# Residual and outputs by 32x32 VectorE transposes instead of TensorE transposes, in a two-layer attention and expert network

## Chip, cores and metric

The kernel runs on one NeuronCore of one Trainium2 chip. The metric is the device time of one execution in microseconds. A NeuronCore has a matrix engine (TensorE, PE in the profile, whose weight loads are listed apart as PEld), a vector engine (VectorE, DVE), an activation engine (ScalarE, ACT), a general engine (GpSimd, POOL) and a queue engine that issues transfers (SyncE, SP). SBUF is the on-chip working memory of 128 partitions, PSUM the memory into which TensorE writes.

## Reference

All arithmetic is float32. The input has 8 batches of 256 channels and 32 x 32 = 1024 positions (tokens). Cut to what matters:

```python
# layer 0: x is (8, 256, 32, 32); 8 heads of 64; softmax over axis 1 (the queries)
xt = x.reshape(B, C, S).transpose(0, 2, 1)
qkv = (xt @ w_qkv + b_qkv).reshape(B, S, 8, 192)
q, k, v = jnp.split(qkv, 3, axis=-1)
attn = softmax(einsum('bihd,bjhd->bijh', q, k) / 8, axis=1)
res = einsum('bijh,bjhd->bihd', attn, v).reshape(B, S, 512)
x = res @ w_out + b_out + xt                  # the residual is the transposed input
# layer 1: t is (8, 1024, 256), token by token
t = t + attention(layer_norm(t), W)           # one head, width 256, softmax over keys
n = layer_norm(t)
t = t + n + top-2-of-8 experts(n)             # each: gelu(n @ w1[e] + b1[e]) @ w2[e] + b2[e]
out = t.transpose(0, 2, 1).reshape(8, 256, 32, 32)
```

Two transposes of whole batches are therefore needed: the input is stored by channels and added as a residual by tokens, and the result is made by tokens and stored by channels.

## The kernel before

Batches are treated one after the other. In `layer0(b)` the input `xT` lies by channels (128 partitions, 2 channel halves, 1024 tokens). Queries and keys of a pair of heads are projected (`project_pair`, L324), and a hand-written order of 32 steps (4 head pairs by 8 blocks of 128 keys) interleaves scores `psc` (L422), the two halves of the column maximum (L437, L446, VectorE), the exponential (L463, ScalarE), the division of the values by the sums (L477, L479, VectorE) and the product `po` (L499). The products of one head pair are copied by ScalarE into `res` (L517), which holds the attention result by channels: 4 groups of 128 channels by 1024 tokens. The projection of a next head pair is put into the steps named in `PROJECT`; the last of these is step (2, 1). To keep `po` in order TensorE waits for empty instructions on another queue (`relay`, L509): POOL for batch 0, SP for the others.

After the steps the residual is formed (L584 to L604): 16 TensorE transposes of 128 x 128 squares of `xT` into two PSUM tiles `pt_x` (L590), two VectorE additions of the bias `b_o` that write `t1` (L593), then for each of 8 blocks of 128 tokens 4 products `pr` of `res` with `wo` (L601, the tokens of the block being the stationary operand) and a VectorE addition to `t1` (L604). Every float32 product shows in the trace as two matmul records and two weight loads; a transpose shows as one of each. `t1` and all that follows from it have the token within its block on the partition, so block `i` holds tokens 128 i to 128 i + 127.

`attend(b)` is the one-head attention of layer 1. Its waits are filled with the first products of the next batch (class `Begin`: `project`, L302, and `values`, L361). `normed(b)` is the second norm, `dispatch(b)` sends the normalised tokens of batches 0 to 6 to rows sorted by expert in device memory. When the steps of layer 0 of batch 7 are done, `experts` runs all sorted blocks. Then batch 7 goes through `attend` and `dense` (all experts for all its tokens) while the class `Results` brings the expert results of the other seven batches back by gathers (L1093), adds them (L1115) and stores them. What is gathered, added and stored at which place is written in the table `PLACES`, as (blocks to add, blocks to gather, halves to store).

`store` (L1145 to L1157) turns a result into the layout of the output: for each channel half it transposes 8 squares on TensorE into a PSUM tile `pout` (L1152), copies them with ScalarE into `oT` (L1154) and sends 512 KB with one transfer (L1155), 128 partitions with 4 KB each. For batch 7 it is called twice, once for each half of the tokens, with 256 KB for each transfer.

A PSUM tile of the kind `big` has three buffers, which `pt_x`, `pout`, the scores, the projections and the transposes of `attend` share; a tile of the kind `acc` has two, shared by `po`, `pr` and `py`.[...]

Of the kernel before, what the change touches and what calls it, by code (L numbers as in the profile page):

```python
# [10 lines left out]
F32 = mybir.dt.float32  # L11
# [8 lines left out]
def kernel(  # L20
# [23 lines left out]
    nc = tc.nc  # L44
# [160 lines left out]
    b1T = const.tile([P, E * NFC], F32, name="b1T")  # L205
    nc.vector.tensor_copy(b1T, ps[:, : E * NFC])

    def bcast(t, n):

        return t.unsqueeze(2).to_broadcast([P, NT, n])  # L210
# [181 lines left out]
    def nothing(*_):  # L392
        pass

    def layer0(b, xT, begun, routing):

# [131 lines left out]
        for at in range(last + LAG + 1):  # L528
            g, j = steps[min(at, last)]

            early = at > LAG and j == 1 and (g, j) not in PROJECT
            if at <= last:
                with tc.issue_after(counted.ins) if counted else nullcontext():
                    score(at, 0, 0)
            if 0 < at <= last + 1:
                with tc.issue_after(counted.ins) if counted else nullcontext():
                    score(at - 1, 1, 1)
                second_max(at - 1, 1)
                soften(at - 1, 1)
            if at >= LAG:  # L540
                with tc.issue_after(counted.ins) if counted else nullcontext():
                    gather_values(at - LAG, 0)
                counted = None
            if at <= last:

                with tc.issue_after(seconds[1].ins) if 1 in seconds else nullcontext():
                    first_max(at, 0)
                score(at, 0, 1)
                score(at, 1, 0)
                second_max(at, 0)  # L550
                if not early:
# [12 lines left out]
            if early:  # L564
                with tc.issue_after(copied[0].ins), tc.issue_after(copied[1].ins):
                    soften(at, 0)
            if at <= last and (g, j) in PROJECT:
                with tc.issue_after(firsts[at, 1].ins), tc.issue_after(array.ins):
                    share(firsts[at, 1])
                    pair, pq, mm = project_pair(b, xT, g + 1)  # L570
                qks.append(pair)
                if g == 0:
                    with tc.issue_after(mm.ins), tc.issue_after(firsts[at, 1].ins):
                        counted = share(pq)
                if b == B - 1 and (g, j) == PROJECT[-1]:
# [5 lines left out]
            pass  # L581


        t1 = one.tile([P, NT, C], F32, tag="t1", name=f"t1_{b}")  # L584
        n = 1024 // C
        for i in range(0, NT, n):
            pt = big(f"pt_x_{b}_{i}")
            for j in range(n):
                for cc in range(NCC):
                    nc.tensor.transpose(  # L590
                        pt[:, j * C + cc * P : j * C + (cc + 1) * P], xT[:, cc, ts(i + j, P)], ident
                    )
            nc.vector.tensor_add(  # L593
                t1[:, i : i + n, :],
                pt.rearrange("p (j c) -> p j c", c=C),
                b_o.unsqueeze(1).to_broadcast([P, n, C]),
            )
        for i in range(NT):
            pr = acc(f"pr_{b}_{i}")
            for g in range(NPAIR):  # L600
                nc.tensor.matmul(  # L601
                    pr[:, :C], res[:, g, ts(i, P)], wo[:, g, :], start=(g == 0), stop=(g == NPAIR - 1)
                )
            nc.vector.tensor_add(t1[:, i, :], pr[:, :C], t1[:, i, :])  # L604
        return t1
# [430 lines left out]
    class Results:  # L1036
# [67 lines left out]
        def add(self):  # L1104
            at = self.added
            if at == len(self.units):
                return
            assert at < self.sent
            self.added += 1
            b, i = self.units[at]  # L1110
            n = at // NT
            gate = self.group.kept[b][0]
            total = self.totals[n]
            for k in range(2):
                nc.vector.scalar_tensor_tensor(  # L1115
                    total[:, i, :],
                    self.slot(at)[:, k, :],
                    gate[:, k, i : i + 1],
                    total[:, i, :],
                    ALU.mult,  # L1120
                    ALU.add,
                )
# [10 lines left out]
        def tick(self, place, behind=None):  # L1133
# [6 lines left out]
                self.gather(behind)  # L1140
            for _ in range(stored):
                if self.whole:
                    b, total, cc = self.whole.pop(0)
                    store(b, total, range(NT), [cc])

    def store(b, total, blocks, ccs=range(NCC)):

        n = len(blocks)
        for cc in ccs:
            pt = big(f"pout_{b}_{blocks[0]}_{cc}")  # L1150
            for at, i in enumerate(blocks):
                nc.tensor.transpose(pt[:, ts(at, P)], total[:, i, ts(cc, P)], ident)  # L1152
            oT = two.tile([P, S], F32, tag="qk1", name=f"oT_{b}_{blocks[0]}_{cc}")
            nc.scalar.copy(oT[:, : n * P], pt[:, : n * P])  # L1154
            nc.sync.dma_start(  # L1155
                out[b, ts(cc, P), blocks[0] * P : (blocks[0] + n) * P], oT[:, : n * P]
            )  # L1157

    def dense(b, t2, tick):

# [71 lines left out]
        def collect(e, n, hT):  # L1232
# [23 lines left out]
            if n == NH2 - 1 and e + NWB < E:  # L1256
                weights(e + NWB)
            if e == E - 1:
                store(b, t2, range(n * (NT // NH2), (n + 1) * (NT // NH2)))

        pending = None
        for at, (e, n) in enumerate((e, n) for e in range(E) for n in range(NH2)):
# [7 lines left out]

    begun = Begin(0, next_x)
    begun.all()
    prepare()
    routing = (nothing(_) for _ in ())
    for b in range(B):
        xT = next_x
        if b + 1 < B:
            next_x = load_x(b + 1)
        t1 = layer0(b, xT, begun, routing)
        if b + 1 < B:  # L1280
            begun = Begin(b + 1, next_x)
            t2 = attend(b, t1, begun.at)
# [52 lines left out]
```

## Time and profile before

| | |
|---|---|
| time, 3 runs | median 2432.24 us (2429.27 to 2434.94) |
| the profiled execution's own time | 2433.04 us |
| its span | 2431.3 us |
| PE busy | 2380.9 us, 98% |
| DVE busy | 1499.5 us, 62% |
| ACT busy | 952.8 us, 39% |
| POOL busy | 381.4 us, 16% |
| transposes of the residual, `pt_x` | 128 of 273 ns each, beside 16 additions of 1219 ns |
| transposes of the outputs, `pout` | 128 of 273 ns each, beside 18 copies (14 of 128 x 1024, 4 of 128 x 512) |
| products `pr` | 512 records of 379 ns, weight loads of 190 ns |
| transfers | 118.65 MB in 57368 packets on the hardware queue |

[...] The profiled execution's own time exceeds its span by 1.7 us, and is 0.8 us above the median of the runs.

### The profile page before, as it was taken

The numbers are of one execution on the slowest core, as the hardware profiler recorded it, in microseconds if no ns is written. First come the engines' busy times: TensorE is split into PE (matmuls) and PEld (weight loads), VectorE is DVE, ScalarE is ACT, GpSimd is POOL, SyncE is SP. The second block draws the span as 40 slices with busy tenths as digits, with TensorE's granted clock in tenths as the row PEclk, the third lists the DMA queues.
The fourth block names the chain that finished last, engine by engine and source line by source line (L and its number), as shares of the span: only waits on it lengthen the run. The fifth ranks groups of instructions, "written<-read, shape, count | busy, mean of one in ns | idle before, by whom it ended". The sixth has DMA issues, their size and how long they took to land.

```text
span 2431.3 us, 37154 instructions
## 1 busy us (share of the span) xinstructions
PE 2380.9 (98%) x14015; PEld 1320.7 (54%) x14015; DVE 1499.5 (62%) x3642; ACT 952.8 (39%) x1587; POOL 381.4 (16%) x383
## 2 busy tenths in 40 slices
PE   9999999999999999999999999999999999999799
PEld 3356534654465336633663356335643588885566
DVE  5674577567755775577557764776478653335543
ACT  3651366126612661166215631563256422221222
POOL 0000011001100010002000200020002144436542
PEclk9999999999999999999999999999999999999899
DMA  7993101000000000000000000000001266663442
GB/s 277 386 384 89 35 19 36 1 18 17 21 18 18 12 25 18 18 8 29 18 2 19 34 18 1 18 34 3 1 18 62 83 218 219 213 207 103 151 148 99
DMA packets 82556, 188.23 MB, mean 77 GB/s; under 512 B 13992, under 2 KB 23880, under 8 KB 80584
## 3 DMA queue, kind: packets, MB, share of 16 engines
q1 hardware_dynamic: 57368, 118.65, 13.5%
q0 software_dynamic: 25008, 67.20, 9.0%
q8 instruction: 111, 1.82, 0.3%
q14 instruction: 69, 0.57, 0.1%
HBM read 100.49 MB, written 110.90 MB: 87 GB/s over the span
## 4 chain that ended last, share of the span: by engine, by line
PE 91%; DVE 3%; ACT 2%; issue 1%; DMA 1%; another core or an unknown queue 1%; SPq 0%; ACTq 0%; DVEq 0%; POOLq 0%
PE psc L422 18%; PE po L499 18%; PE py L661 9%; PE ps L635 7%; PE pqk L324 7%; PE pr L601 5%; PE pv L361 4%; PE ph L982 4%; PE pe L1007 4%; PE pdy L1238 2%; PE px L620 2%; PE pqk L302 2%; PE pa L654 2%; PE pdh L1214 2%; PE pt_n L234 1%
## 5 line engine op out<-in xcount | busy, mean ns | idle before, releaser
L463 ACT ACTIVATE ex<-psc,nmax 128x1024 f32<-128x1024 f32 x512 | 570.0, 1114 | 305.0 <-DVE scrap L446 221.8
L422 PE MATMUL psc<-qk,qk 64*64 64x512 f32 x4096 | 574.7, 592 | 4.4 <-ACT ex L463 4.4
L499 PE MATMUL po<-ex,vs 64*64 64x512 f32 x4096 | 570.2, 591 | 3.8 <-DVE vs L479 3.0
L446 DVE TENSOR_SCALAR_CACHE_REDUCE scrap<-psc,nmax 128x512 f32<-128x512 f32 x512 | 384.5, 751 | 178.8 <-PE psc L422 152.4
L437 DVE TENSOR_REDUCE nmax<-psc 128x1 f32<-128x512 f32 x512 | 350.6, 685 | 9.3 <-PE psc L422 9.3
L422 PEld LDWEIGHTS psc<-qk,qk 64*64 64x64 f32 x4096 | 179.9, 132 | 280.2 <-ACT ex L463 133.6
L499 PEld LDWEIGHTS po<-ex,vs 64*64 64x64 f32 x4096 | 175.3, 132 | 273.2 <-DVE vs L479 80.5
L661 PE MATMUL py<-n,aT 128*128 128x256 f32 x1024 | 238.4, 386 | 6.8 <-DVE aT L656 4.0
L635 PE MATMUL ps<-nT,xa 128*128 128x512 f32 x512 | 236.0, 592 | 0.0
L661 PEld LDWEIGHTS py<-n,aT 128*128 128x128 f32 x1024 | 191.8, 191 | 70.9 <-DVE aT L656 42.0
L845 POOL DMA_INDIRECT rows<-n,d_at x112 | 108.8, 971 | 705.9 <-DVE nmax L437 703.4
L646 ACT ACTIVATE ex<-ps,nmax 128x1024 f32<-128x1024 f32 x64 | 71.3, 1113 | 351.5 <-DVE nmax L643 306.6
L776 POOL TENSOR_TENSOR t<-t,n 128x2048 f32<-128x2048 f32 x8 | 36.3, 4535 | 1032.0 <-issue 766.8
L324 PE MATMUL pqk<-xT,wqkv 128*128 128x512 f32 x384 | 171.2, 599 | 0.0
L666 DVE SCALAR_TENSOR_TENSOR t<-py,rs,t 128x256 f32<-128x256 f32 x64 | 30.9, 483 | 206.3 <-PE py L661 206.3
L635 PEld LDWEIGHTS ps<-nT,xa 128*128 128x128 f32 x512 | 93.5, 190 | 81.2 <-issue 75.1
L1093 POOL DMA_INDIRECT yk<-y,yat x112 | 108.5, 969 | 108.4 <-DVE t L1247 39.5
L324 PEld LDWEIGHTS pqk<-xT,wqkv 128*128 128x128 f32 x384 | 71.0, 190 | 99.8 <-issue 77.8
L289 ACT ACTIVATE qk<-pqk,b_qks 128x512 f32<-128x512 f32 x124 | 85.6, 690 | 96.2 <-PE pqk L324 79.9
L361 PE MATMUL pv<-wqkv,xT 128*128 128x512 f32 x256 | 119.7, 597 | 0.2 <-ACT wqkv L106 0.2
L643 DVE TENSOR_REDUCE nmax<-ps 128x1 f32<-128x1024 f32 x64 | 78.3, 1223 | 61.4 <-PE ps L635 58.5
L601 PE MATMUL pr<-wo,res 128*128 128x256 f32 x512 | 111.8, 379 | 0.0
(193 smaller groups left out, 2499.1 us busy)
## 6 DMA issues: line engine op xcount, KB each, us to landing
rows<-wb SPq DMA_DIRECT2D x7, 8192.0 KB
y<-yb SPq DMA_DIRECT2D x63, 256.0 KB
xT<-in_x_dram SPq DMA_DIRECT2D x7, 1024.0 KB
sums<-t SPq DMA_DIRECT2D x7, 1024.0 KB
o<-sums SPq DMA_DIRECT2D x7, 1024.0 KB
out_dram<-oT SPq DMA_DIRECT2D x14, 512.0 KB
wpack<-in_L_ffn_w_dram SPq DMA_DIRECT2D x4, 1024.0 KB
wb<-in_L_ffn_w_dram SPq DMA_DIRECT2D x16, 256.0 KB
```

The costliest lines, as they stand in the source:

```text
L324: mm = nc.tensor.matmul(pq[:, ts(n, 512)], wqkv[:, cc, t, ts(g, P)], xT[:, cc, ts(n, 512)], start=(cc == 0), stop=(cc == NCC - 1),)
L361: nc.tensor.matmul(pv, self.xT[:, cc, ts(i, P)], wqkv[:, cc, 2, :], start=(cc == 0), stop=(cc == NCC - 1),)
L422: mm = nc.tensor.matmul(pss[at, h][ts(c, DK), ts(n, 512)], k[r, j * P + c * DK : j * P + (c + 1) * DK], q[r, ts(n, 512)], start=True, stop ...
L437: firsts[at, h] = nc.vector.tensor_reduce(nmax, pss[at, h][:, ts(0, 512)], AX.X, ALU.max, negate=True)
L446: seconds[h] = nc.vector.tensor_scalar(scrap, pss[at, h][:, ts(1, 512)], -1.0, nmaxes[at, h], ALU.mult, ALU.min, accum_out=nmax,)
L463: nc.scalar.activation(ex, pss.pop((at, h)), AF.Exp, bias=nmaxes.pop((at, h)), scale=1.0, accum_out=sums[at][:, h : h + 1],)
L499: mm = nc.tensor.matmul(po[n][ts(h, DK), :], vss[at][keys, h, :], exps[at, h][keys, ts(n, 512)], start=(j == 0 and turn == 0), stop=(j == ...
L601: nc.tensor.matmul(pr[:, :C], res[:, g, ts(i, P)], wo[:, g, :], start=(g == 0), stop=(g == NPAIR - 1))
L635: nc.tensor.matmul(psc[:, ts(n, 512)], xa[:, ec, ts(i, P)], nT[:, ec, ts(n, 512)], start=(ec == 0), stop=(ec == NCC - 1),)
L661: nc.tensor.matmul(py[:, :D], aT[:, ts(m, P)], n1[:, m, :], start=(m == 0), stop=(m == NT - 1))
L845: scatter = nc.gpsimd.indirect_dma_start(out=view[:, :], out_offset=bass.IndirectOffsetOnAxis(ap=ats[k][:, i : i + 1], axis=0), in_=n2[:, ...
L1093: ins = nc.gpsimd.indirect_dma_start(out=self.slot(at)[:, k, :], out_offset=None, in_=self.group.y[:, :], in_offset=bass.IndirectOffsetOnAxis(
```

## The change

The 256 TensorE transposes are gone, with the ScalarE copies and the PSUM tiles that belonged to them. VectorE transposes instead, an instruction of 128 x 1024 elements that transposes each 32 x 32 square within its group of 32 partitions. What such squares leave undone (moving a square to other partitions) is done by the transfers, and the order of the tokens within a half batch is changed so that transfers find runs of 128 tokens (512 bytes): partition 32 a + p of block `i` in half `n` holds token 512 n + 128 a + 4 p + i.

- `load_squares(b)` loads the input a second time, with 8 transfers of 128 KB (32 partitions by 8 by 128 elements), into the buffer that `attend` uses as `xa`.
- `residual(b, xs)` makes `t1` with two VectorE transposes, which read every fourth element of `xs`, and adds the bias with one POOL addition of 128 x 2048 elements. It is called in step (2, 1), behind the first maximum of that step.
- The stationary operand of `pr` is `own(res[:, g, :], i)`: 128 tokens at a distance of 4 elements (16 bytes), where it was 128 adjacent ones.
- `store(b, total, n)` stores one half of the tokens with one VectorE transpose, which writes every fourth element of `oT`, and four transfers of 128 KB.
- In `PLACES` the stores that stood at "last weights", "last products" and "norm 2" stand at ("mixed", 3) to ("mixed", 6), one half each.

```diff
+    NB = NT // NH2
+    SQ = 32
+    NQ = P // SQ
+    def own(t, i):
+        return t.rearrange("c (n p i) -> c n i p", n=NH2, i=NB)[:, i // NB, i % NB, :]
...
+    def load_squares(b):
+        xs = one.tile([P, C // SQ, NH2, P], F32, tag="xa", name=f"xs_{b}")
+        src = x[b].rearrange("(g c) (n a k) -> a n c g k", c=SQ, n=NH2, a=NQ)
+        for a in range(NQ):
+            for n in range(NH2):
+                nc.sync.dma_start(xs[ts(a, SQ), :, n, :], src[a, n])
+        return xs
+    def residual(b, xs):
+        t1 = one.tile([P, NT, C], F32, tag="t1", name=f"t1_{b}")
+        for n in range(NH2):
+            nc.vector.transpose(
+                t1[:, ts(n, NB), :].rearrange("p i (g c) -> p i g c", c=SQ),
+                xs[:, :, n, :].rearrange("p g (t i) -> p i g t", i=NB),
+            )
+        nc.gpsimd.tensor_add(t1, t1, b_o.unsqueeze(1).to_broadcast([P, NT, C]))
+        return t1
...
                 qks.append(pair)
+                if (g, j) == PROJECT[-1]:
+                    with tc.issue_after(firsts[at, 1].ins):
+                        t1 = residual(b, xs)
...
-        t1 = one.tile([P, NT, C], F32, tag="t1", name=f"t1_{b}")
-        n = 1024 // C
-        for i in range(0, NT, n):
-            pt = big(f"pt_x_{b}_{i}")
-            for j in range(n):
-                for cc in range(NCC):
-                    nc.tensor.transpose(
-                        pt[:, j * C + cc * P : j * C + (cc + 1) * P], xT[:, cc, ts(i + j, P)], ident
-                    )
-            nc.vector.tensor_add(
-                t1[:, i : i + n, :],
-                pt.rearrange("p (j c) -> p j c", c=C),
-                b_o.unsqueeze(1).to_broadcast([P, n, C]),
-            )
         for i in range(NT):
             pr = acc(f"pr_{b}_{i}")
             for g in range(NPAIR):
                 nc.tensor.matmul(
-                    pr[:, :C], res[:, g, ts(i, P)], wo[:, g, :], start=(g == 0), stop=(g == NPAIR - 1)
+                    pr[:, :C], own(res[:, g, :], i), wo[:, g, :], start=(g == 0), stop=(g == NPAIR - 1)
                 )
...
-            **{("mixed", i): (3, 2, 0) for i in range(1, 7)},
-            "last weights": (0, 0, 2),
-            "last products": (0, 0, 1),
+            **{("mixed", i): (3, 2, 1 if i > 2 else 0) for i in range(1, 7)},
             ("mixed", 7): (0, 2, 0),
-            "norm 2": (0, 0, 1),
...
-                self.whole += [(b, total, cc) for cc in range(NCC)]
+                self.whole += [(b, total, n) for n in range(NH2)]
...
-    def store(b, total, blocks, ccs=range(NCC)):
-        n = len(blocks)
-        for cc in ccs:
-            pt = big(f"pout_{b}_{blocks[0]}_{cc}")
-            for at, i in enumerate(blocks):
-                nc.tensor.transpose(pt[:, ts(at, P)], total[:, i, ts(cc, P)], ident)
-            oT = two.tile([P, S], F32, tag="qk1", name=f"oT_{b}_{blocks[0]}_{cc}")
-            nc.scalar.copy(oT[:, : n * P], pt[:, : n * P])
-            nc.sync.dma_start(
-                out[b, ts(cc, P), blocks[0] * P : (blocks[0] + n) * P], oT[:, : n * P]
-            )
+    def store(b, total, n):
+        oT = two.tile([P, D // SQ, P], F32, tag="qk1", name=f"oT_{b}_{n}")
+        nc.vector.transpose(
+            oT.rearrange("p g (t i) -> p i g t", i=NB),
+            total[:, ts(n, NB), :].rearrange("p i (g c) -> p i g c", c=SQ),
+        )
+        dst = out[b].rearrange("(g c) (n a k) -> n a c g k", c=SQ, n=NH2, a=NQ)
+        for a in range(NQ):
+            nc.sync.dma_start(dst[n, a], oT[ts(a, SQ)])
...
     begun.all()
+    xs = load_squares(0)
     prepare()
...
+        if b > 0:
+            xs = load_squares(b)
-        t1 = layer0(b, xT, begun, routing)
+        t1 = layer0(b, xT, begun, routing, xs)
```

More of the change, by code (lines that the diff above doesn't have):

```diff
@@ L393, in nothing, with layer0 @@
         pass
-    def layer0(b, xT, begun, routing):
+    def load_squares(b):
[14 more added lines that the diff above has]
+        return t1
+    def layer0(b, xT, begun, routing, xs):
         v, qks = begun.v, begun.qks
@@ L1142, in tick @@
                 if self.whole:
-                    b, total, cc = self.whole.pop(0)
-                    store(b, total, range(NT), [cc])
-    def store(b, total, blocks, ccs=range(NCC)):
-        n = len(blocks)
-        for cc in ccs:
-            pt = big(f"pout_{b}_{blocks[0]}_{cc}")
-            for at, i in enumerate(blocks):
-                nc.tensor.transpose(pt[:, ts(at, P)], total[:, i, ts(cc, P)], ident)
-            oT = two.tile([P, S], F32, tag="qk1", name=f"oT_{b}_{blocks[0]}_{cc}")
-            nc.scalar.copy(oT[:, : n * P], pt[:, : n * P])
-            nc.sync.dma_start(
-                out[b, ts(cc, P), blocks[0] * P : (blocks[0] + n) * P], oT[:, : n * P]
-            )
+                    b, total, n = self.whole.pop(0)
+                    store(b, total, n)
+    def store(b, total, n):
[7 more added lines that the diff above has]
+            nc.sync.dma_start(dst[n, a], oT[ts(a, SQ)])
     def dense(b, t2, tick):
@@ L1258, in collect @@
             if e == E - 1:
-                store(b, t2, range(n * (NT // NH2), (n + 1) * (NT // NH2)))
+                store(b, t2, n)
         pending = None
```

## The prediction

> **What bounds the kernel now.** First the page's busy times and its chain of waits.
>
> ```profile
> PE 2380.9 (98%) x14015; PEld 1320.7 (54%) x14015; DVE 1499.5 (62%) x3642; ACT 952.8 (39%) x1587; POOL 381.4 (16%) x383
> ...
> PE 91%; DVE 3%; ACT 2%; issue 1%; DMA 1%; another core or an unknown queue 1%; SPq 0%; ACTq 0%; DVEq 0%; POOLq 0%
> ```
>
> TensorE is the path: 91% of the chain. What is taken off it counts unless a wait is beneath; transfers and POOL matter only through waits. Next the timeline where batch 1 leaves layer 0 (start, duration, engine, line; brackets are idle time).
>
> ```profile
> 416.50 0.44 PE L590 MATMUL pt_x<-ident,xT 128*128 128x128 f32 x2
> ...
> 417.26 2.32 PE L499 MATMUL po<-ex,vs 64*64 64x512 f32 x16 [0.32 <-DVE vs L479]
> ...
> 419.52 1.75 PE L590 MATMUL pt_x<-ident,xT 128*128 128x128 f32 x14
> 419.63 1.08 ACT L517 COPY res<-po 128x512 f32<-128x512 f32 x2 [2.99 <-PE po L499]
> ...
> 421.10 3.19 PE L601 MATMUL pr<-wo,res 128*128 128x256 f32 x14
> ```
>
> Fourteen residual transposes fill 419.52 to 421.10, but the copies of `po` to `res` run beneath them. Then the timeline of step (2, 1), batch 1, where the residual goes.
>
> ```profile
> 357.54 7.13 PE L324 MATMUL pqk<-xT,wqkv 128*128 128x512 f32 x16
> ...
> 357.86 0.68 DVE L437 TENSOR_REDUCE nmax<-psc 128x1 f32<-128x512 f32 x1
> ...
> 365.76 0.75 DVE L446 TENSOR_SCALAR_CACHE_REDUCE scrap<-psc,nmax 128x512 f32<-128x512 f32 x1 [7.22 <-PE psc L422]
> ```
>
> VectorE has a hole of 7.22 us there, behind the maximum that `residual` is placed after. The last stage, by the timeline:
>
> ```profile
> 2256.33 1.91 PE L1152 MATMUL pout<-ident,o 128*128 128x128 f32 x16
> 2265.21 1.76 PE L654 MATMUL pa<-ident,ex 128*128 128x128 f32 x7 [6.97 <-ACT oT L1154]
> ...
> 2330.61 1.91 PE L1152 MATMUL pout<-ident,o 128*128 128x128 f32 x16
> 2332.36 3.60 PE L1214 MATMUL pdh<-n2T,wb 128*128 128x512 f32 x8
> ```
>
> Sixteen output transposes take 1.75 us from a dense stream (109 ns each); once TensorE also waits 6.97 us for the copies that free PSUM. Last, rows of the groups by shape, for costs:
>
> ```profile
> L601 PEld LDWEIGHTS pr<-wo,res 128*128 128x128 f32 x512 | 96.7, 190 | 12.8
> L688 PEld LDWEIGHTS pl<-n2T,rT 128*32 128x32 f32 x128 | 3.3, 111 | 7.7 <-DVE n2T L235 5.3 <-DVE o L1115 0.8 <-issue 0.4
> ...
> L816 DVE TENSOR_TENSOR d_rows<-d_rows,counts 128x64 f32<-128x64 f32 x6 | 1.3, 224 | 0.2
> L810 DVE TENSOR_TENSOR d_rows<-d_upto,d_per 128x64 f32<-128x64 f32 x7 | 1.9, 276 | 0.2
> L799 DVE COPY d_per<-d_cn 128x64 f32<-128x64 f32 x7 | 1.4, 207 | 0.0
> ```
>
> L810 writes at a distance of 32 bytes and takes 52 ns more than L816, which writes adjacent elements: 0.8 ns per element on top of one. L799 reads at that distance and takes 207 ns, less than either.
>
> [...]
>
> **The change part by part**, against the profiled execution's own 2433.0 us.
>
> *Residual off TensorE.* Without `pt_x`, `pr` still needs the PSUM buffer that the first `res` copy frees: it ends at 419.63 + 0.54 = 420.17, with a signal about 420.33. So `pr` starts 0.77 us earlier instead of 1.58. The instruction order of the new kernel puts four passes of the next batch's projection (0.215 us each, 0.87 us) around the last `po`, into the wait. But these passes came after `pr` and covered the norm: in the timeline of batch 1 `pt_n` starts at 440.07, straight after the projections, and the last `n` (L224, 437.11 + 2.67) is ready at 439.78: no slack. What is pulled forward is missed there. I take 0.77 x 8 = 6.2 us gained (13 if the norm chain gives way, 0 if the copies' wait grows).
>
> *Residual on VectorE.* Two transposes of 1024 elements: [...]like L593 (1.22 us), or about 2 us if the 16-byte reads cost what L810's writes do. 2.4 to 4 us fit in the hole of 7.22 us. The POOL addition costs 4.54 us by L776, the same shape; it ends by 367.1 at the latest if the transposes run 358.6 to 362.6, before the next two-input VectorE instruction, L479 at 368.32. `t1` is needed 55 us later; expert scatters wait behind the addition on POOL, and nobody waits for them soon. Batch 0: the order-keeping empty instructions stand behind it on POOL; with TensorE 6 us in the projection, 0.5 us (0 to 3). Batch 7: `plan` already fills the hole (TensorE waits 0.8 us for its last instruction, L906), so both transposes are exposed: 3 us (2.4 to 4).
>
> *Loading squares.* 8 MB more in all, on transfer engines that the page shows under 20% busy in these stages. SP issues the 8 transfers once the previous `attend` is through with `xa`, when the empty instructions of the new batch are not yet due; the data has 80 us to land. Nothing.
>
> *The strided weight load of `pr`.* This is the large unknown: 512 loads. The matmuls step at 0.2155 us, the load beneath takes 190 ns. From 32 to 128 columns it rises by 79 ns, 0.83 ns per column, so 107 of the 190 are columns. If columns cost nothing more, the load stays hidden. If the column part doubles, as L810's writes do, a full load takes 297 ns; its column part of 214 is still under the step if loads overlap one another (the transposes' loads of 141 ns at steps of 109 show that they can), and it adds (297 - 216) x 512 = 42 us if not. [...]Below nothing is excluded, since the load is already hidden. I take 2 us, because reads at a distance cost little in L799 and half rate just fits.
>
> *Outputs off TensorE.* In `dense` 80 of the 112 transposes lie in the dense stream: 80 x 0.109 = 8.7 us. In the last `attend` the first 16 cost 1.75 and the wait 6.97; the second 16 lie beneath VectorE's `aT` and save nothing. Part of the wait has a releaser that the profile doesn't know, so I take 7.5 of 8.7 us (2 to 10).
>
> *Outputs on VectorE.* Four transposes go into ("mixed", 3 to 6), beside 6.7 us of VectorE work per block (two of 1.22, six additions of 0.494, small ones of 1.25 in all) and 7.75 us of TensorE (8 x 0.109 + 8 x 0.43 + 16 x 0.2155): 1.22 or 2.1 us more make 7.9 to 8.8. They stand after `aT`, which TensorE awaits, and before the next maximum, which has a step's slack: 1 us lost in all (0 to 4). In `dense` VectorE idles over 4 us per step. Each store issues 4 transfers instead of 1 (0.34 us each on SP): hidden.
>
> *Around the gates.* Without copies ScalarE's order changes: a first Gelu slips ahead of the exponential of the gates, with table loads of 1.28 us. That chain ends in `pg`, for which TensorE waits 2.48 us already: 1.5 us (0 to 3).
>
> *The end.* The chain shows 0.44 + 0.53 us of transposes for the first half of batch 7 within the last products; they go (0.97). The last store trades 0.87 us of transposes and two copies of 0.5 us for one VectorE transpose (1.2 to 2.1 us), four issues instead of two, and packets of 512 bytes instead of 2 KB: 2 us lost, 1 net (0 to 3).
>
> *Sum:* -6.2 + 0.5 + 3 + 2 - 8.7 - 7.5 + 1 + 1.5 + 1 = -13.4, to 2433.0 - 13.4 = 2419.6; the median stands 0.8 lower: 2419.
>
> **Rivals.** *A, the forecast:* 2419. With the bounds of its small terms 2407 to 2429. *B, the gain drowns:* the waits beneath persist: `attend` keeps its 7 us in another place, the boundary gains nothing. -8.7 of `dense` against the 9 us of costs above: 2432. For it: most of the gaps in that stage have unknown releasers; against it: the dense stream is without idle time. *C, weight loads don't overlap:* `pr` steps at 297 ns, 2419 - 2 + 42 = 2459, slower. It decides from 248 ns on, where 512 x 32 ns eat the gain. For it: the cost of L810. Against: a half-rate column part is 214 ns. *D, [...]:* 2419 - 2 + 109 = 2526. For it: nothing reads weights in steps in this trace, so it is open; against: L799.
>
> **How the numbers follow.** A 0.57, B 0.11, C 0.19, D 0.13. No change is within 0.2%, 4.9 us, about what a measurement can tell. A lies wholly below 2427 but for little: faster 0.60 with the part of B that keeps the wait's gain; same 0.06; slower 0.34 (C, D, a little of B). The predicted time is A's. A's own range is 2407 to 2429; for 8 in 10 the range must take in B and most of C: 2407 to 2465. D is left out above.
>
> **What would show it.** The start-to-start step of `pr`: 0.2155 us says A, about 0.3 C, over 0.4 D; its loads' mean in the groups: under 300 ns fits A or C. The VectorE transposes' mean: 1.2 or 2. The window of step (2, 1): no TensorE idle time except in batch 7. TensorE's time from the last `po` to `pt_n`: 0.8 us shorter. `pdh` following `pdy` without a gap in `dense`, and no wait of 7 us at the last two blocks of `attend`. I am wrong if the `pr` stage grows by more than 2 us per batch, or if VectorE's transposes take over 3.5 us and overflow their hole.

## The result, and the profile after

The change takes 2423.06 us (median of 6 runs, 2419.51 to 2426.44) where the kernel before, run beside it, takes 2433.37 us (6 runs, 2429.27 to 2435.03): a ratio of 0.9957, interval 0.9946 to 0.9968, some 10 us. The profiled execution of the change took 2419.76 us, its span is 2418.1 us, 13.2 us less than that of before. The forecast of 2419 us was 4 us low. Most of its terms were not right, though, and the experiments were made to find out which.

The page of the change, busy times and the chain of waits:

```profile
PE 2363.3 (98%) x13759; PEld 1315.7 (54%) x13759; DVE 1546.1 (64%) x3658; ACT 939.3 (39%) x1570; POOL 419.0 (17%) x391
...
PE 91%; DVE 5%; ACT 2%; issue 1%; another core or an unknown queue 1%; DMA 1%; SPq 0%; DVEq 0%; ACTq 0%; POOLq 0%
```

256 matmul records are gone, and TensorE is busy 17.6 us less; VectorE's share of the path rose from 3% to 5%. Its groups by shape (line, engine, operation, shape, count | busy us, mean ns | idle us before) show what was bought and what it cost:

```profile
L619 PE MATMUL pr<-wo,res 128*128 128x256 f32 x512 | 121.6, 398 | 0.3 <-ACT res L546 0.3
L619 PEld LDWEIGHTS pr<-wo,res 128*128 128x128 f32 x512 | 120.7, 331 | 3.7 <-ACT res L546 3.7
...
L417 DVE STREAM_TRANSPOSE t<-xs 128x1024 f32<-128x1024 f32 x16 | 32.0, 2064 | 0.0
...
L1164 DVE STREAM_TRANSPOSE oT<-o 128x1024 f32<-128x1024 f32 x14 | 28.6, 2040 | 0.2
```

The weight loads of `pr` take 331 ns instead of 190, and each VectorE transpose about 2 us, the upper of the two values that the prediction considered. The timeline where batch 1 leaves layer 0 (TensorE alone):

```profile
416.42 2.35 PE L528 MATMUL po<-ex,vs 64*64 64x512 f32 x16
418.70 1.13 PE L311 MATMUL pqk<-xT,wqkv 128*128 128x512 f32 x2
419.66 15.18 PE L619 MATMUL pr<-wo,res 128*128 128x256 f32 x64
434.67 1.88 PE L311 MATMUL pqk<-xT,wqkv 128*128 128x512 f32 x4
436.39 1.88 PE L370 MATMUL pv<-wqkv,xT 128*128 128x512 f32 x4
438.11 1.93 PE L243 MATMUL pt_n<-ident,n 128*128 128x128 f32 x16
```

Passes of the next projection (`pqk`) now fill the wait for the copies of `po`. The 64 records of `pr` start at a distance of (434.67 - 419.66) / 64 = 0.2345 us instead of 0.2155. So the loads of 331 ns overlap one another here, but not without cost: 19 ns for each of 512 records, 9.7 us in all. Batch 7 in step (2, 1), where VectorE also runs `plan`, a chain of small instructions that lays out the experts' blocks; first the kernel before, then the change:

```profile
1856.73 0.17 DVE L877 TENSOR_TENSOR_SCAN p_ends<-ones,p_blocks 128x8 f32<-128x8 f32 x1
...
1861.62 0.19 DVE L906 CAST row_at<-p_lo 128x63 int32<-128x63 f32 x1
```

```profile
1852.04 4.04 DVE L417 STREAM_TRANSPOSE t<-xs 128x1024 f32<-128x1024 f32 x2
...
1856.22 4.73 POOL L421 TENSOR_TENSOR t<-t,b_o 128x2048 f32<-128x2048 f32 x1 [2.85 <-issue]
...
1857.02 3.96 DVE L895 TENSOR_TENSOR_SCAN p_ends<-ones,p_blocks 128x8 f32<-128x8 f32 x1
...
1865.70 0.20 DVE L924 CAST row_at<-p_lo 128x63 int32<-128x63 f32 x1
...
1867.91 1.99 PE L451 MATMUL psc<-qk,qk 64*64 64x512 f32 x8 [6.07 <-ACT ex L492]
```

The scan of 8 elements took 0.17 us before and takes 3.96 us here; it ends 0.03 us after POOL's addition (1860.98 against 1860.95 us). The plan ends at 1865.9, 14.8 us after TensorE began the projection of this step (1851.1), where before it took 7.1 us (1854.8 to 1861.8): 4 us of transposes and 3.8 us of the scan. TensorE waits 6.07 us for what stands behind it. In the other batches the same pieces are hidden, as in step (2, 1) of batch 1:

```profile
357.33 3.99 DVE L417 STREAM_TRANSPOSE t<-xs 128x1024 f32<-128x1024 f32 x2
...
361.46 4.54 POOL L421 TENSOR_TENSOR t<-t,b_o 128x2048 f32<-128x2048 f32 x1 [2.80 <-issue]
...
364.62 0.75 DVE L475 TENSOR_SCALAR_CACHE_REDUCE scrap<-psc,nmax 128x512 f32<-128x512 f32 x1 [3.30 <-PE psc L451]
```

VectorE still idles 3.30 us of its hole of 7.22. In the last stage, from the norm of batch 7 to `pg`, the view of waits (total, times, longest, in us) gives for TensorE:

```profile
PE pt_n L243 <- DVE rstd_f L231: 4.0, 1, 4.0
PE py L679 <- DVE aT L674: 3.7, 2, 2.7
PE plT L729 <- ACT lT L714: 3.1, 1, 3.1
PE py L679 <- issue: 2.6, 1, 2.6
```

The wait of 6.97 us for `oT` is gone, but waits of similar kinds remain.

The two traces compared by stretches, from the starts of the same products; the prediction's terms are put where they belong. A boundary is the passage from layer 0 of a batch to its norm. A second pair was taken later on one chip (below).

| stretch (us, change minus before) | predicted | first pair | second pair |
|---|---|---|---|
| start to the norm of batch 6 (7 boundaries) | -3.2 | -4.1 | -3.7 |
| from there to the last `po` of batch 7 (the plan) | +3.0 | +8.8 | +9.4 |
| from there to the norm of batch 7 (last boundary, experts) | -0.5 | -2.0 | +0.6 |
| from there to `pg` (last `attend`, gates) | -5.0 | -6.0 | -3.2 |
| from `pg` to the end | -7.7 | -9.9 | -11.3 |
| sum | -13.4 | -13.2 | -8.2 |

### The profile page after: what moved, and what is told of

Its sections match the earlier page's. It is cut to its first block, busy times and chain, and to the rows that moved or that the text cites. A ratio compares the mean times of both kernels' runs of the same rounds, so it can differ in the third digit from the quotient of the medians.

```text
span 2418.1 us, 36817 instructions
## 1 busy us (share of the span) xinstructions
PE 2363.3 (98%) x13759; PEld 1315.7 (54%) x13759; DVE 1546.1 (64%) x3658; ACT 939.3 (39%) x1570; POOL 419.0 (17%) x391
## 4 chain that ended last, share of the span: by engine, by line
PE 91%; DVE 5%; ACT 2%; issue 1%; another core or an unknown queue 1%; DMA 1%; SPq 0%; DVEq 0%; ACTq 0%; POOLq 0%
PE po L528 19%; PE psc L451 18%; PE py L679 9%; PE ps L653 8%; PE pqk L333 7%; PE pr L619 5%; PE ph L1000 4%; PE pe L1025 4%; PE pv L370 4%; PE px L638 2%; PE pdy L1251 2%; PE pa L672 2%; PE pdh L1227 2%; PE pqk L311 2%; PE px L990 1%
## 5 line engine op out<-in xcount | busy, mean ns | idle before, releaser
L619 PEld LDWEIGHTS pr<-wo,res 128*128 128x128 f32 x512 | 120.7, 331 | 3.7 <-ACT res L546 3.7
L619 PE MATMUL pr<-wo,res 128*128 128x256 f32 x512 | 121.6, 398 | 0.3 <-ACT res L546 0.3
```

What stands on the lines that cost most here:

```text
L619: nc.tensor.matmul(pr[:, :C], own(res[:, g, :], i), wo[:, g, :], start=(g == 0), stop=(g == NPAIR - 1))
```

## The experiments

The theory after the first reading: the strided weight loads cost 9.8 us, POOL's addition beside the plan another 4, and the rest of the gain is what the TensorE transposes were worth. Each run below has its own runs of the kernel before on its chip; times are medians, and the chips differ (the kernel before took 2433.8 us beside the first four, 2418.1 beside the next four, 2432.8 beside the last four), so ratios are compared.

### Runs of adjacent tokens

The token of partition 32 a + t in block i becomes 128 a + 32 i + t within its half. The copy out of PSUM puts the tokens in that order, and all else reads and writes adjacent elements. This kernel is called e1_runs below.

```diff
-        return t.rearrange("c (n p i) -> c n i p", n=NH2, i=NB)[:, i // NB, i % NB, :]
+        return t[:, ts(i, P)]
...
-                xs[:, :, n, :].rearrange("p g (t i) -> p i g t", i=NB),
+                xs[:, :, n, :].rearrange("p g (i t) -> p i g t", i=NB),
...
-                copied = [nc.scalar.copy(res[:, g, ts(n, 512)], po[n]) for n in range(NH2)]
+                copied = [
+                    nc.scalar.copy(
+                        res[:, g, ts(n, 512)].rearrange("c (i a t) -> c a i t", i=NB, a=NQ),
+                        po[n].rearrange("c (a i t) -> c a i t", i=NB, a=NQ),
+                    )
+                    for n in range(NH2)
+                ]
...
-            oT.rearrange("p g (t i) -> p i g t", i=NB),
+            oT.rearrange("p g (i t) -> p i g t", i=NB),
```

> All of the change stays, but blocks of tokens are made of runs of 32 adjacent tokens instead of every fourth one: both VectorE transposes then read and write adjacent elements, and the copies of po to res write the tokens in the order in which the weight loads of pr read them, so these read adjacent elements. Theory 1 (the loads of pr cost more because of the distance of 16 bytes): loads back from 331 to about 190 ns, the step of pr from 0.2345 to 0.2155 us, 512 x 0.019 = 9.8 us less, 2413 us; if the distance also makes the VectorE transposes long (2.06 us), they fall to about 1.2 us and the plan of batch 7 and the end give another 2 us, 2411. Rival (the step of pr grew for another reason, such as a lower clock or the evictions): step stays at 0.2345, 2423 us. For the transposes: near 2.06 us means that fp32 squares cost that by themselves, near 1.2 that the distance does.

Measured: 2412.10 us, 0.9916 of before (0.9900 to 0.9933). The groups of this kernel by shape:

```profile
L625 PEld LDWEIGHTS pr<-wo,res 128*128 128x128 f32 x512 | 97.2, 190 | 16.7 <-ACT res L547 3.7
L547 ACT COPY res<-po 128x512 f32<-128x512 f32 x64 | 34.2, 588 | 28.9 <-PE po L528 28.9
...
L417 DVE STREAM_TRANSPOSE t<-xs 128x1024 f32<-128x1024 f32 x16 | 18.9, 1219 | 0.0
L1170 DVE STREAM_TRANSPOSE oT<-o 128x1024 f32<-128x1024 f32 x14 | 17.3, 1237 | 0.2
```

The loads are back at 190 ns, and the transposes take 1.22 and 1.24 us, about the duration of the addition that the lower estimate was read from (L593, 1.22 us). So a distance of 16 bytes is what cost 141 ns per load, 0.84 us per transpose when reading (L417) and 0.80 when writing. The reordered copy takes no longer than before: 588 ns in both kernels.

### Adjacent weights alone

```diff
-        return t.rearrange("c (n p i) -> c n i p", n=NH2, i=NB)[:, i // NB, i % NB, :]
+        return t[:, ts(i, P)]
```

> The change as it is, but pr reads its weights from adjacent tokens again, with the transposes' distance of 16 bytes kept. (The attention part of a token then meets the residual of another token: the computation is changed there.) Theory 1: pr's loads 190 ns, step 0.2155 us, 9.8 us less than with the change: 2413 us, with the VectorE transposes unchanged at 2.06 us. Rival (something other than the distance in the loads): loads 331 ns, 2423 us.

Measured: 2412.62 us, 0.9918 (0.9904 to 0.9933), with loads of 190 ns and transposes of 2058 and 2034 ns. This and the kernel above are equal within the intervals, so nearly all of the 10 us between the change and them is the weight loads, and the rival falls. What the shorter transposes of e1_runs bring is too little for the times to tell. In the traces it is 0.8 us in batch 7 (the stretch with the plan is 7.8 us longer than before in e1_runs, 8.6 here) and 0.8 us at the end (from the last `pdy` 7.4 us instead of 8.2); elsewhere none of it shows.

### Residual alone

`store`, the list of halves and `PLACES` as before the change, all else as in the change. The store of before doesn't undo the change's order of tokens.

```diff
-    def store(b, total, n):
+    def store(b, total, blocks, ccs=range(NCC)):
...
-            **{("mixed", i): (3, 2, 1 if i > 2 else 0) for i in range(1, 7)},
+            **{("mixed", i): (3, 2, 0) for i in range(1, 7)},
+            "last weights": (0, 0, 2),
+            "last products": (0, 0, 1),
...
+            "norm 2": (0, 0, 1),
```

> Residual by squares alone; outputs are transposed by TensorE as before (the tokens of the outputs come in another order). From the measured parts: the boundary gains 0.60 us in each of 8 batches (-4.8), pr costs +9.8, the plan of batch 7 about +6: slower than before by 11, 2444 us. By the prediction's own terms (-6.2 + 0.5 + 3 + 2) it would be 2433. If the gain that was seen came mostly from the residual, it would be under 2425.

Measured: 2440.03 us, 1.0026 (1.0014 to 1.0039): 6 us slower than before, where 11 were expected and the prediction's terms would give none. The expected loss was too large: the gain at the boundary is larger than the 0.60 us that the expectation took from the wait alone (see the point-by-point part).

### The addition written behind the plan

```diff
+                        if b < B - 1:
+                            bias(t1)
...
                         plan(groups[0])
+                        bias(t1)
```

> The change as it is, but in batch 7 POOL's addition of the bias comes after the plan, the VectorE transposes still ahead of it. Theory (POOL's addition and VectorE instructions with two SBUF inputs exclude each other): the scan p_ends falls from 3.96 to about 0.17 us, TensorE's wait at psc from 6.07 to about 2.3 us, 3.8 us less than with the change: 2419 us. Rival (the plan is late only because 4 us of transposes stand ahead of it): the wait stays near 6 us, 2423 us.

Measured: 2423.23 us, 0.9960 (0.9945 to 0.9975), as the change. The run says nothing about the theory: nothing in the data makes the addition wait for the plan, and POOL ran it as soon as the transposes were done, as the timeline of batch 7 shows:

```profile
1856.39 4.74 POOL L424 TENSOR_TENSOR t<-t,b_o 128x2048 f32<-128x2048 f32 x1 [2.83 <-issue]
...
1857.20 3.97 DVE L900 TENSOR_TENSOR_SCAN p_ends<-ones,p_blocks 128x8 f32<-128x8 f32 x1
```

### The addition made to wait for the plan

```diff
-                        plan(groups[0])
+                        planned = plan(groups[0])
+                        tc.add_manual_dep(bias(t1).ins, planned.ins.name, BEHIND)
```

> e1_runs, and in batch 7 POOL's addition of the bias now truly waits for the last instruction of the plan (in e4_add_after_plan it had only been written behind the plan, and ran at the same moment as before, so that run told nothing). Theory (POOL's addition and VectorE instructions with two SBUF inputs exclude each other): the scan p_ends falls from 3.96 to about 0.17 us and the plan ends some 3.8 us earlier; but the addition then lies beside the next vs of VectorE (a product of two SBUF inputs), which should stretch to 2 to 4 us in its turn, so that the time falls by between 0 and 3.8 us from 2412: 2408 to 2412. Rival (the scan is long for a reason of its own or because the queue of VectorE is long): the scan stays at 3.96 us.

Measured: 2394.86 us, 0.9911 (0.9897 to 0.9924), beside 0.9916 for the kernel that it was made from. The timeline of batch 7:

```profile
1846.81 0.17 DVE L906 TENSOR_TENSOR_SCAN p_ends<-ones,p_blocks 128x8 f32<-128x8 f32 x1
...
1852.62 4.53 POOL L424 TENSOR_TENSOR t<-t,b_o 128x2048 f32<-128x2048 f32 x1
...
1854.15 3.16 DVE L510 TENSOR_TENSOR vs<-v,rs 128x128 f32<-128x128 f32 x1
...
1857.37 1.09 PE L530 MATMUL po<-ex,vs 64*64 64x512 f32 x8 [2.36 <-DVE vs L510]
```

The scan is 0.17 us again and `vs`, 0.29 us elsewhere, is stretched to 3.16 us in its place, ending 0.16 us after POOL. The reductions of PSUM that ran on VectorE between the addition's start and `vs` kept their 0.7 us. So the stretch follows POOL's addition: moving it frees the scan (0.17 us) and stretches the two-input instruction that then lies beside it (`vs`, 3.16 us). TensorE's waits in e1_runs and here:

```profile
1857.94 1.99 PE L451 MATMUL psc<-qk,qk 64*64 64x512 f32 x8 [4.39 <-ACT ex L492]
```

```profile
1853.91 1.09 PE L453 MATMUL psc<-qk,qk 64*64 64x512 f32 x8 [0.60 <-ACT ex L494]
```

The 4.39 us behind the plan have become 0.60 there and the 2.36 at `po`. In the trace the stretch with the plan is 5.0 us longer than before, where it was 7.8; a gain in time over e1_runs is not shown, the ratios being equal within their intervals.

### The residual of batch 7 one step earlier

Made from e1_runs, and called e6_residual_earlier below.

```diff
-                if (g, j) == PROJECT[-1]:
+                if (g, j) == PROJECT[-1 if b < B - 1 else -2]:
```

> e1_runs, with the residual of batch 7 (transposes and POOL's addition) one projection step earlier, at (1, 1), where no plan stands; the other batches as in e1_runs. Theory (the plan of batch 7 pays for the transposes ahead of it and for POOL's addition beside it): the scan is 0.17 us again, TensorE's wait at psc behind the plan falls from about 6 us to about that of the kernel before, where the last wait there was 0.8 us, and the 7 to 8 us by which batch 7 fell behind come back: 2405 us. Rival (the loss of batch 7 has other causes, such as the lower clock seen after the wait): 2410 to 2412.

Measured: 2392.70 us, 0.9896 (0.9881 to 0.9912): the lowest ratio of the study together with the last variant below, though its interval overlaps that of e1_runs, so a gain over e1_runs is not shown by the times. In the trace the scan takes 0.17 us and the wait behind the plan is gone. From the norm of batch 6 to the last `po` this kernel falls behind the one before by 4.2 us, where e1_runs fell behind by 7.8. Left over is a stretch of the same kind with another victim, at (1, 1), where the expert routing of batch 6 runs; `d_rows`, 0.23 us in the kernel before, takes 4.54 us here and ends 0.09 us after POOL's addition:

```profile
1811.77 4.51 POOL L421 TENSOR_TENSOR t<-t,b_o 128x2048 f32<-128x2048 f32 x1 [49.26 <-DVE t L417]
...
1811.83 4.54 DVE L835 TENSOR_TENSOR d_rows<-d_rows,d_cn 128x64 f32<-128x64 f32 x1
...
1821.18 1.56 PE L451 MATMUL psc<-qk,qk 64*64 64x512 f32 x8 [2.40 <-ACT ex L492]
```

The next variant has the same code in this stretch and falls behind by only 2.5 us: there the wait is 2.42 us, but the records of `psc` and `po` after it take 1.09 and 1.04 us, here 1.56 and 1.95. So half to two thirds of the theory's 7 to 8 us came in the traces.

### The gates before the first Gelu

e6_residual_earlier, with the first Gelu of `dense` ordered behind the exponential of the gates, which saves a table load (1.28 us in the traces) within their chain.

```diff
-                now = (e, n, hidden(e, n))
+            with tc.issue_after(exped[0].ins) if at == 0 else nullcontext():
+                now = (e, n, hidden(e, n))
```

> e6_residual_earlier, and the first Gelu of the dense stage is ordered behind the exponential of the gates. Theory (the Gelu that slipped ahead cost the chain of the gates a table load of 1.28 us): about 1.2 us less than e6_residual_earlier, pg's wait on all_gates shorter by as much. Rival (pg waits for VectorE's additions, not for the table): no difference between the two.

Measured: 2392.75 us, 0.9900 (0.9885 to 0.9915): no difference. The timeline of this kernel tells what the gates wait for:

```profile
2259.24 5.04 DVE L1138 SCALAR_TENSOR_TENSOR o<-yk,gate,o 128x256 f32<-128x256 f32 x1
...
2259.46 4.52 POOL L802 TENSOR_TENSOR t<-t,n 128x2048 f32<-128x2048 f32 x1
...
2264.20 0.21 DVE L740 COPY g_l<-plT 128x64 f32<-128x64 f32 x1
...
2269.67 1.87 PE L1217 MATMUL pg<-ident,all_gates 128*8 128x128 f32 x8 [5.30 <-DVE all_gates L1211]
```

One more VectorE addition with two SBUF inputs (0.47 us elsewhere) stretched to 5.04 us by a POOL addition, that of `t + n`, which the kernel before has too (2.32 us there). `g_l` stands behind it. TensorE's wait at `pg` is 5.29 us without and 5.30 us with the edit. The run rightly shows no gain for this pair of kernels, but it can't tell of the change itself: in e6_residual_earlier too the table was loaded before `g_l` was made, and the exponential ran 0.04 us after its operand was made. In the change it waited longer (see *Gates* below).

### Outputs alone, and the four corners on one chip

The kernel before with the change's `store`, `PLACES` and list of halves:

```diff
-                self.whole += [(b, total, cc) for cc in range(NCC)]
+                self.whole += [(b, total, n) for n in range(NH2)]
...
-                store(b, t2, range(n * (NT // NH2), (n + 1) * (NT // NH2)))
+                store(b, t2, n)
```

> The kernel before with the outputs by squares alone: residual and the weight loads of pr stay as before (the tokens of the outputs come in another order). From the difference between the change and e3_residual_alone, 2423 - 2440 = -17, and from the stretches of the change's trace (6.0 us less from the last attend's norm to pg, 9.9 less from pg to the end): 2433.5 - 16.5 = 2417 us. Rival (the two parts help one another, and one alone gives less): 2421 or more.

Measured: 2407.95 us, 0.9963 (0.9949 to 0.9977), 10 us less than before, not the 17 that the change minus the residual alone had given. Either the parts act on one another, or times from different chips can't be subtracted, or the difference is noise: the two intervals behind the 17 leave anything from 11 to 23 us. So before, change, residual alone and outputs alone were run on one chip.

> The kernel before, run beside the next three on one chip, so that the four corners (neither part, residual, outputs, both) and their traces can be compared without a change of chip. In the runs so far the outputs gave -17 us by subtraction (2423 - 2440) on one chip and -10 alone (2408 - 2418) on another, where every kernel was some 15 us quicker. Theory G: the chips differ in the last attend, where VectorE waits for gathered rows; from its norm (pt_n) to pg the trace of before had 114 us; on a chip with early rows it should have under 105, with the waits of aT, t and rs on other things than TensorE and ScalarE gone, and all other stretches equal within 2 us. Rival: the chips differ everywhere, by the granted clock; then the stretches differ in proportion.

> The change itself on the same chip. Theory G: where rows land early, before minus change is smaller in the last attend (0 to 4 us instead of 6), since its 7 us wait on the copies is smaller there; in all 2423 of 2433 on a chip of the first kind, 2408 to 2412 of 2418 on one of the second kind.

> Residual by squares alone (the tokens of the outputs come in another order). By the stretches up to the last attend, which no chip changed: +4 to +6 us against before. Parts that add (theory): change minus this equals outputs alone minus before within 4 us. Rival (the parts act on one another): they differ by 6 us or more, as the subtraction over two chips suggests.

> Outputs by squares alone (the tokens of the outputs come in another order). Theory of parts that add: 2417 of 2433 on a chip of the first kind, 2408 of 2418 on one of the second. Of this, 8 to 10 us from pg to the end on either kind, the rest in the last attend.

| on one chip | time, us | ratio (interval) |
|---|---|---|
| before | 2432.15 | 1.0002 (0.9994 to 1.0010) |
| change | 2424.08 | 0.9965 (0.9952 to 0.9978) |
| residual alone | 2436.41 | 1.0015 (1.0008 to 1.0023) |
| outputs alone | 2419.62 | 0.9949 (0.9935 to 0.9963) |

The ratios are to 2432.75 us, the median of all runs of the kernel before on this chip. The parts add: +3.7 and -13.1 give -9.5, against -8.7 for the change, far from the 6 us or more by which the rival wanted them to differ. So the output part wins some 13 us here, 10.8 of them from `pg` to the end, and the residual part as it was made loses 4. Change minus residual alone is -12.3 on this chip. The residual alone came out a little below the 4 to 6 us that were expected of it, outputs alone 3 us above the expected 2417.

Outputs alone ran on two chips, and its two traces differ by 9.4 us of span (2417.4 and 2408.0). The norm of batch 7 starts at 2186.3 and 2185.8, and from `pg` to the end both have 121.6 us. From that norm to `pg` it is 109.5 and 100.6 us: all but 0.5 us of the difference. TensorE's waits there, on the slower chip and then on the quicker one:

```profile
PE py L665 <- DVE aT L660: 4.6, 4, 2.5
PE pt_n L238 <- DVE n L228: 4.0, 1, 4.0
PE py L665 <- issue: 3.6, 1, 3.6
```

```profile
PE pt_n L238 <- DVE n L228: 3.9, 1, 3.9
PE py L665 <- DVE aT L660: 2.9, 2, 2.6
```

and VectorE's own waits on the slower chip begin with one that the quicker one doesn't have:

```profile
DVE t L670 <- remote: 8.2, 2, 5.1
```

That the last `attend` is where these two runs of one program differ is shown, and with it that the gain there is no property of the change alone. That VectorE waits for gathered rows in these places, as theory G has it, is not: the trace names no releaser ("remote"). The kernel before has no trace from the quicker chip, so the under 105 us that theory G asked of it stays untested.

## Why the prediction held, point by point

The time was right by luck: the gain at the boundary and the cost of the weight loads were both taken far too small and nearly cancel, and the loss in batch 7, also taken too small, is made up for in part by a larger gain in `dense`. Of the large terms only that of the outputs came near.

*Residual off TensorE, -6.2: too small, by half.* The prediction let only the 0.77 us at the copies of `po` count, since it took `pt_n` to need the last normalised block ("no slack"). (The 0.16 us for the signal in that term was the author's estimate; in the change `pr` starts 0.26 us after the first copy's end, at 419.66 after 419.40 us.) The step to "no slack" failed: `pt_n` transposes block after block, and needs only the first block to start. The lines of batch 1, before and in e1_runs, whose loads cost nothing extra:

```profile
437.11 2.67 DVE L224 TENSOR_SCALAR n<-t,mv_a,rstd_a 128x256 f32<-128x256 f32 x8 [0.20 <-DVE rstd_a L222]
440.07 1.15 PE L234 MATMUL pt_n<-ident,n 128*128 128x128 f32 x9
```

```profile
434.58 2.67 DVE L233 TENSOR_SCALAR n<-t,mv_a,rstd_a 128x256 f32<-128x256 f32 x8 [0.20 <-DVE rstd_a L231]
435.82 1.92 PE L243 MATMUL pt_n<-ident,n 128*128 128x128 f32 x16
```

The first transpose of `pt_n` starts 2.96 us after the eight blocks of `n` begin in the kernel before, and 1.24 us after that in e1_runs: 1.72 us of slack were used. From the end of the last `po` to `pt_n` the time falls from 20.48 to 18.14 us, 0.62 of it before `pr` and these 1.72 after it: the passes pulled forward were not missed. The prediction also had their size wrong. The four 512-column records of the projection cost 0.43 us each (in the change four take 1.72 us, from 434.67 to 436.39), not 0.215 us, which is the step of the 256-column records of `pr`; so 1.72 us were pulled forward, not 0.87. The next stretches give 0.5 to 0.8 us back, 0.4 of that between `pt_n` and the gates of the same batch. Net, e1_runs gains 1.65 us per batch (from -2.47 at the first norm to -12.38 at the seventh), so some 12 to 13 us for 8 batches. The prediction had named 13 "if the norm chain gives way"; that the figure is met is again partly chance, since the passes cost twice what it took and a part was given back. In the change itself the same stretch is 1.14 us shorter, near the 0.8 that the prediction had named as a sign: the gain of 2.34 less 1.2 for the loads.

*Strided weight load of `pr`, +2: too small, 9.7 measured.* The prediction chose 2 because the column part would double and stay just under the step. That is the step that failed. The doubling was an estimate from L810's 0.8 ns more per element, beside the 1.05 ns per element that the maxima of the kernel before show (L437: 685 ns for 512 elements, L643: 1223 ns for 1024). By the rows that the prediction shows, 79 ns for 96 columns, 105 of the 190 ns are columns (it wrote 107). If the rest is constant, the column part at 331 ns is 246, an estimate from these rows: more than double, and above the old step of 215.5. The step became 234.5, so the load binds, but below the load's length and below this column part; what sets 234.5 is not shown. Neither rival was it: C would have had the step equal the load, D a step of over 400 ns (its 109 us were an assumption of the author's, not shown by the trace). At a distance of 16 bytes VectorE's transpose pays for reads as for writes (0.84 and 0.80 us), which the 207 ns of L799 had hidden: that instruction reads only 64 elements, with no adjacent copy of its shape beside it, and the prediction gave it too much weight against L810's 276 ns.

*Residual on VectorE:* hidden in seven batches, as forecast, at the upper value of 2 us. Batch 0's 0.5 us on POOL didn't show. The plan of batch 7 was the worst term: 3 predicted, some 8 measured (8.8 less the 0.5 to 0.8 that each batch gives back here): both transposes were exposed, as forecast, and the stretched scan came on top. The prediction checked POOL's addition against the next two-input instruction of an ordinary batch, L479, and not against the plan's own. Four places show what that costs: the scan, `vs`, `d_rows` and `o` took 3.96, 3.16, 4.54 and 5.04 us beside POOL additions of 4.5 to 4.7, and 0.17, 0.29, 0.23 and 0.47 elsewhere; each ended 0.03 to 0.30 us after POOL's. In the change a reduction with one SBUF input, `p_blocks` (L893), runs beside the same addition as the scan and keeps its 0.39 us. `p_below` (L886), with two SBUF inputs, had started 0.05 us before that addition and keeps its 0.39 us too, while the addition takes 4.73 us instead of 4.54. In three of the four places POOL's record starts first, by 0.80, 1.53 and 0.06 us. In the fourth VectorE's record starts at 2259.24 us, 0.22 us before POOL's, and is stretched all the same; why is open.

*Outputs off TensorE.* In `dense` and at the end 7.7 predicted, 9.9 and 11.3 measured. 88 transposes at 0.109 us (80 in the stream, 8 among the last products) are 9.6; the bias products `pb` ran 1.5 us shorter in the first pair, and the granted clock was 0.96 in place of 0.95 in that stretch. The end itself is 2.3 us longer (last `pdy` to the end of the span: 8.1 instead of 5.9), where 2 had been taken. In the last `attend` with the gates 5 predicted, 6.0 and 3.2 measured; outputs alone gained 1.9 there on the one chip. The 7 us wait did go, but it was partly cover for others: `pt_n` waits 4.0 us in place of 2.5, and `py` on `aT` still 3.7. Rival B was right for part of this stage.

*Gates, +1.5:* right for the chain of the gates. The Gelu did slip ahead with its table loads (1.28 us each), as the order of instructions had told. VectorE's wait for the exponential of the gates, before and in the change (view of waits, last `attend` to `pg`):

```profile
DVE g_z L725 <- ACT g_p L722: 0.3, 1, 0.3
```

```profile
DVE g_z L743 <- ACT g_p L740: 2.3, 1, 2.3
```

From `plT` to `pg` the change takes 9.7 us and before 8.1 us (9.6 and 8.1 in the second pair). TensorE's wait at `pg` is the same in the first pair, 2.45 us and 2.48, and 1.5 us longer in the second, 2.30 and 0.78, so how much of it reached the time stays open. In e6_residual_earlier it is hidden: the table is loaded by 2265.43 us, and `g_l` starts only at 2266.66, behind the `o` that was stretched to 4.65 us beside POOL's addition.

*Sum.* Too little gain at the boundary (by 6 us), too little cost in `pr` (8) and in batch 7 (5), too little gain in `dense` (2 to 4): these nearly cancel, and the net error is that of the time, a few us. With the loads at 331 ns the prediction's own warning, `pr` growing by more than 2 us per batch, did not come true (1.2), so its test could not tell that the term was wrong by a factor of five.

## What to carry to other kernels

A layout that spares a transpose should put the stride where nothing on the path reads it: here one reordered ScalarE copy out of PSUM, at no cost (588 ns in both orders), let the weight loads (190 ns instead of 331) and VectorE transposes (1.22 to 1.24 us instead of 2.04 to 2.06) find adjacent elements and gave about as much as the change itself; nearly all of that came from the weight loads. When work moves to POOL, look at every VectorE instruction with two SBUF inputs that can fall beside it, above all at short ones in a dependent chain: here four of 0.17 to 0.47 us took 3.16 to 5.04 beside additions of 4.5 to 4.7. And a consumer that works block by block needs only the first block to start: its slack is counted from there (1.72 us of it were used here).

## What was not expected of the hardware

- A float32 weight load of 128 columns at a distance of 16 bytes takes 331 ns (190 adjacent), yet a stream of such loads with 256-column products steps at 234.5 ns (215.5 adjacent).
- VectorE's transpose of 128 x 1024 float32 elements takes 1.22 to 1.24 us with adjacent elements and 2.04 to 2.06 at a distance of 16 bytes, on the read side or the write side.
- One program, run on two chips, differed by 8.9 us in one stage of 100 to 110 us, and by 0.5 us in all the rest together.
- After TensorE's wait of 6.07 us in batch 7 the next records took 1.99 us where 1.04 is usual, and the granted clock was 0.87 from 1867 to 1887 us, where the kernel before, without the wait, has 1.00 (1862 to 1882): the loss there was more than the wait. It isn't so after every wait: of two kernels with the same code in one stretch, the records after a wait of 2.4 us were slow in one (1.56 and 1.95 us) and not in the other (1.09 and 1.04).
